# A new order for the last three groups of a planned kernel: by the path that each operation has left, instead of group by group

## The chip, the cores and the metric

The kernel runs on one core of a Trainium2 chip. The metric is the device time of one launch in microseconds (us), a median of several runs. A core has five engines with instruction streams of their own: TensorE (PE in the profile, with its weight loads as PEld), VectorE (DVE), ScalarE (ACT), GpSimd (POOL) and SyncE (SP), which here only issues DMA transfers. Each engine takes its instructions strictly in the order in which the program lists them; between engines they wait for each other by semaphores. So the order of the list is a thing that can be tuned by itself.

## The reference

The input x has 128 graphs of 64 nodes with 256 features (8192 rows of 256 floats), and all share one 64x64 adjacency matrix. Four layers follow, each on a normalised input and added to x:

```
h = relu(layernorm(x));  x = x + layer0(h, adj)   # two graph convolutions, then LSTMs over windows of 1..4 graph nodes
h = relu(layernorm(x));  x = x + layer1(h, adj)   # normalised Laplacian, 4-head masked attention, Gelu MLP, layer norms
h = relu(layernorm(x));  x = x + layer2(h, adj)   # graph attention: softmax of leaky relu of s1 + s2, masked
h = relu(layernorm(x));  x = x + layer3(h, adj)   # U^T h, a two-layer MLP, U h; U = eigenvectors of a Laplacian of adj
```

Layer 1 needs the largest eigenvalue of adj, and layer 3 all eigenvectors of a matrix made from it. Both depend on adj alone. No row of one graph meets another graph's rows after layer 0's windows are closed within the graph, so the work can be cut into groups of graphs freely.

## The kernel before

The kernel records every operation first, with the buffers that it reads and writes, and gives each a group number. Group -1 is the set-up, groups 0 to 7 are layer 0 on eight parts of x, 8 and 9 load the weights of the later layers, and groups 10 to 25 are layers 1 to 3 on sixteen parts of 512 rows each. The eigen-decomposition is a group of its own, set aside, and fills gaps of the other engines during layer 0.

```python
NT, GT, HT = 64, 8, 4                  # (put together) tiles of 128 rows; tiles of a layer-0 group; tiles of a later group
NG = NT // GT                          # 8
NEARLY = 6
ORDER = [g % NG for g in range(NG - NEARLY, 2 * NG - NEARLY)]
SETUP, WEIGHTS, ATTN, REST, EIG = -1, NG, NG + 1, NG + 2, 1000
...
    for i, g in enumerate(ORDER):
        plan.group = REST + 2 * i
        x = X[g]
        if g < len(put):
            x = load(back[g], put[g])
        for h in range(GT // HT):
            plan.group = REST + 2 * i + h
            xh = x[:, h * HT:(h + 1) * HT, :]
            layer1(xh)
            layer2(xh)
            layer3(xh)
            SP.dma_start(xout[g * GT // HT + h], xh)
    plan.issue()
```

Then a planner plays the recorded operations through with a modelled cost for each, and writes down the order in which they start; that order is the program. At each step it looks on every engine at the operations whose inputs are there. One that can start at once comes before one that has to wait, and among those that can start at once the rank decides, the smallest first:

```python
    def schedule(self):
        for op in reversed(self.ops):
            op.path = op.lat + max((o.path for o in op.after), default=0.0)
        ...
        while len(order) < len(self.ops):
            oldest = min(left)
            best = None
            for e, ops in ready.items():
                pick = None
                for op in ops:
                    if op.group != self.aside and op.group >= oldest + self.window(oldest):
                        continue
                    t = max(now[e], op.ready)
                    ...                # and a free buffer of each kind, some kept back for the oldest group
                    rank = (t > now[e] + 1e-9, t if t > now[e] + 1e-9 else 0.0, self.rank(op))
                    if pick is None or rank < pick[0]:
                        pick = (rank, t, op)
                if pick and (best is None or pick[1] < best[1]):
                    best = pick
            ...

    def rank(self, op):
        if op.group == self.aside:
            return (-2 if op.eng == "PE" else 1000, op.index)
        return (op.group, -op.path, op.index)
```

`op.path` is the length of the longest chain of operations that starts with this one, in modelled us: what is left to the end along that chain. So an operation of an older group always goes first, and within one group the one with the longest chain. How many groups may be open at once, and what is kept back for the oldest, is set here:

```python
    def window(oldest):
        return max(oldest, 0) + 2 - oldest if oldest < NG - 1 else max(oldest, REST) + 6 - oldest

    def reserve(kind, oldest):
        if oldest < NG:
            return {"big": 4, "mid": 6, "stat": 1, "attn": 0, "bank": 3}[kind]
        return {"big": 6, "mid": 0, "stat": 2, "attn": 1, "bank": 2}[kind]
```

With the oldest unfinished group at 10 or later, six groups are open. The kinds are buffers: "big" is a wide one in SBUF (128 x 1032 floats), "stat" holds statistics, "attn" a block-diagonal attention matrix, and "bank" is one of the eight PSUM banks. The list of big buffers grows as places fall free; each place is named with the groups that must be done before:

```python
NBIG, NMID, NSTAT, NATTN = 8, 8, 14, 4
    ...
    more(arena[:, (NG - NEARLY) * GT * D:], (EIG,))
    more(whh[3], tuple(range(NG)))
    more(mids, tuple(range(NG)))
    ...
    for i, g in enumerate(ORDER[:NEARLY]):
        more(places[g % NEARLY], (REST + 2 * i, REST + 2 * i + 1))
```

The three layers of one group, cut to their stages (every line stands for several instructions; the first layer is by far the longest):

```python
    def layer1(x):
        h = relu_norm(x); lx = mix_fm(h, lapb)                      # VectorE, GpSimd, ScalarE; then 16 products on TensorE
        x1 = tm(); ... proj_tm(lx, Wc); norm(x1); ...
        x1T = to_fm(x1)                                             # transposes on TensorE
        qT, kT, v = ...                                             # 3 projections
        ps = [bank("qk") for m in range(2)]
        with plan.burst(): ...                                      # 32 products of 64x64, one unbroken run
        s = ...; softmax; pT = fm(); ...                            # Exp on ScalarE, transposes
        with plan.burst(): ...                                      # 32 products of 64x64
        x2 = ... Wo ...; norm(x2); x2T = ...                        # projection, layer norm, transposes
        mT = ... AF.Gelu ...                                        # W1, Gelu on ScalarE
        ps = proj_tm(mT, W2, 4, t0); ...; norm(x2); x += ...        # W2, layer norm

    def layer2(x):
        hT = to_fm(relu_norm(x)); wh = tm(HT, D + 2); ...           # transposes, projection to 258 columns
        V.tensor_mul(s2d, ...); PE.matmul(ps, same, flat(s2d)); ... # the sum s1 + s2
        V.tensor_scalar(e2, e, 0.2, ...); softmax; Exp; transposes
        ... PE.matmul(..., pT, wh) ...; x += ...

    def layer3(x):
        h = relu_norm(x); aT = mix_fm(h, Ub)
        hid = ... W3a ...; uT = ... UTb ...; x += ... W3b ...
```

Of the kernel before, what the change touches and what calls it, by code (L numbers as in the profile page):

```python
# [19 lines left out]
class Virt:  # L20
# [3 lines left out]
    def __init__(self, val, ap, path=()):  # L24
        self.val, self.ap, self.path = val, ap, path
# [41 lines left out]
class Plan:  # L67
# [5 lines left out]

    SLACK = {"PE": 0.12, "V": 0.05, "ACT": 0.05, "G": 0.05, "SP": 0.05}

    def __init__(self, tc, engines, pools, late, reserve, window, aside):

        self.tc, self.engines, self.pools, self.late = tc, engines, pools, late
        self.reserve, self.window, self.aside = reserve, window, aside
        self.ops, self.group, self.seen = [], 0, {}
        self.run, self.whole = None, False

# [129 lines left out]
    def schedule(self):  # L215
# [17 lines left out]
# [9 lines that stand above are left out]
                    need = {}  # L242
                    for v in op.vals:
                        if v.buf is None:
                            need[v.kind] = need.get(v.kind, 0) + 1
                    for k, c in need.items():
                        spare = 0
                        if op.group != oldest:
                            spare = max(0, self.reserve(k, oldest) - held.get((k, oldest), 0))
                        times = sorted(free[k].values())  # L250
                        t = max(t, times[c - 1]) if len(times) >= c + spare else None
                        if t is None:
                            break
                    if t is None:
# [6 lines that stand above are left out]
# [44 lines left out]
    def rank(self, op):  # L305
        if op.group == self.aside:
            return (-2 if op.eng == "PE" else 1000, op.index)
        return (op.group, -op.path, op.index)

    def issue(self):  # L310
        real = lambda a: a.real() if isinstance(a, Virt) else a
# [540 lines left out]
NT = 64  # L852
GT = 8
NG = NT // GT
HT = 4
# [3 lines left out]
SETUP, WEIGHTS, ATTN, REST, EIG = -1, NG, NG + 1, NG + 2, 1000  # L859
# [37 lines left out]
def gnn_kernel(ctx: ExitStack, tc: tile.TileContext, a, out):  # L897
    nc = tc.nc
# [3 lines left out]
    def C(shape, name):  # L902
        return pool.tile(list(shape), F32, name=name)
# [6 lines left out]
    pools = {  # L910
        "big": [C([P, HT * (D + 2)], f"big{i}") for i in range(NBIG)],
        "mid": [mids[:, i * 512:(i + 1) * 512] for i in range(NMID)],
        "stat": [C([P, HT * 10], f"stat{i}") for i in range(NSTAT)],
        "attn": [wih[3][:, i * HT * P:(i + 1) * HT * P] for i in range(NATTN)],
        "bank": [psum.tile([P, 512], F32, name=f"bank{i}") for i in range(8)],
    }
    late = {("attn", i): (ATTN,) for i in range(NATTN)}
# [17 lines left out]
            return {"big": 4, "mid": 6, "stat": 1, "attn": 0, "bank": 3}[kind]  # L935
        return {"big": 6, "mid": 0, "stat": 2, "attn": 1, "bank": 2}[kind]

    plan = Plan(tc, {"PE": nc.tensor, "V": nc.vector, "ACT": nc.scalar, "G": nc.gpsimd, "SP": nc.sync}, pools, late, reserve, window, EIG)
    PE, V, ACT, G, SP = (plan.proxy(e) for e in ("PE", "V", "ACT", "G", "SP"))

    def bank(name):
# [587 lines left out]
```

## Time and profile before

The median of three runs is 2389.2 us (2388.43 to 2390.73). The profiled execution has a span of 2386.6 us and 33035 instructions.

| engine | busy, us | share of the span | instructions |
|---|---|---|---|
| PE (TensorE) | 2291.3 | 96% | 11288 |
| PEld (its weight loads, beside PE) | 1604.7 | 67% | 11288 |
| DVE (VectorE) | 1742.6 | 73% | 6943 |
| ACT (ScalarE) | 974.9 | 41% | 1939 |
| POOL (GpSimd) | 458.5 | 19% | 448 |

All operations are issued by one line of the planner (line 316), so the rows of the profile are told apart by engine, by shape and by the names of the buffers, and not by line. "arena", "x", "mids", "Wih" and "Whh" are places in SBUF: weights and parts of x of layer 0 lay there first, and the buffers and weights of the later layers take the places over. So a name tells where an operand lies and not what it is; the shape and the number of instructions tell that. One float32 product shows as two matmul instructions, a transpose as one. In rows of the timeline the columns are the start, the duration, engine, line, operation, output and input, the partitions and columns, the number of instructions merged, and in square brackets the idle time of the engine before them with what ended it. "PEclk", or the granted clock, is the share of its full clock that TensorE was given.

### The profile page before, as it was taken

The page shows a single profiled execution, that of the slowest core. Times are in us where ns is not written, and L with a number is a line of the kernel's source. Part 1 is how long each engine was busy: PE and PEld are TensorE (multiplying, and loading weights), DVE is VectorE, ACT ScalarE, POOL GpSimd, SP SyncE. Part 2 cuts the span into 40 slices and gives each one's busy share as a digit, 9 for nine tenths or more (in the row PEclk, how much of TensorE's full clock was granted, in tenths as well). Part 3 has the DMA queues.
Part 4 walks back from the last instruction along what each step waited for, and adds up shares of the span by engine and source line. Part 5 has one row for each costly group of instructions (what it writes and reads, how often), then busy time and mean ns, then how long its engine had stood idle before and what let it go on. Part 6 is the DMA issues. An engine that isn't in the chain of part 4 may idle for free. (4 is left out here: it accounts for less than half of the span.)

```text
span 2386.6 us, 33035 instructions
## 1 busy us (share of the span) xinstructions
PE 2291.3 (96%) x11288; PEld 1604.7 (67%) x11288; DVE 1742.6 (73%) x6943; ACT 974.9 (41%) x1939; POOL 458.5 (19%) x448
## 2 busy tenths in 40 slices
PE   8999999999999999999999999999999999999885
PEld 6577477478477477576576577767767777677664
DVE  7656657667999999999886236678568768867653
ACT  3333433433333433333333423555545455545442
POOL 2101001001001001001001023234244433533321
PEclk9999999999999999999999999999999999999998
DMA  6000001000000000000000110000000001000000
GB/s 238 1 1 18 1 1 54 0 1 1 1 1 1 1 1 1 1 1 5 1 1 3 36 35 1 1 10 10 10 18 10 1 27 36 10 10 9 10 10 18
DMA packets 27384, 35.44 MB, mean 15 GB/s; under 512 B 3280, under 2 KB 24656, under 8 KB 26704
## 3 DMA queue, kind: packets, MB, share of 16 engines
q1 hardware_dynamic: 27216, 33.34, 4.2%
q8 instruction: 89, 1.46, 0.3%
q14 instruction: 79, 0.65, 0.1%
HBM read 22.85 MB, written 10.49 MB: 14 GB/s over the span
## 5 line engine op out<-in xcount | busy, mean ns | idle before, releaser
L316 PE MATMUL bank<-big,Wih 128*128 128x256 f32 (+2 forms) x2592 | 867.5, 476 | 7.2 <-DVE Wih L316 2.1
L316 PEld LDWEIGHTS bank<-big,Wih 128*128 128x128 f32 x2592 | 480.6, 191 | 280.9 <-issue 164.7
L316 ACT ACTIVATE mids<-bank,bl 128x256 f32<-128x256 f32 (+2 forms) x624 | 344.5, 563 | 618.0 <-PE bank L316 608.9
L316 PE MATMUL bank<-big,Whh 128*128 128x256 f32 (+2 forms) x1440 | 453.0, 449 | 0.0
L316 DVE TENSOR_TENSOR arena<-arena 64x21 f32<-64x21 f32 (+6 forms) x2317 | 377.1, 193 | 35.4 <-POOL arena L316 1.1
L316 PEld LDWEIGHTS bank<-big,Whh 128*128 128x128 f32 x1440 | 269.1, 190 | 119.1 <-issue 61.5
L316 POOL TENSOR_TENSOR stat<-stat,mhalf 128x4 f32<-128x4 f32 x112 | 116.2, 1038 | 727.8 <-DVE stat L316 726.0
L316 DVE TENSOR_TENSOR big<-big,mids 128x256 f32<-128x256 f32 (+2 forms) x192 | 93.9, 489 | 156.3 <-ACT mids L316 155.1
L316 DVE TENSOR_TENSOR big<-mids 128x512 f32<-128x512 f32 (+2 forms) x244 | 139.8, 579 | 32.2 <-ACT mids L316 28.1
L316 ACT ACTIVATE mids<-big 128x256 f32<-128x256 f32 (+2 forms) x176 | 89.9, 511 | 133.5 <-DVE big L316 78.2
L316 PE MATMUL bank<-Wih,big 128*128 128x256 f32 (+2 forms) x552 | 134.3, 389 | 0.8 <-ACT big L316 0.5
L316 DVE TENSOR_SCALAR arena<-arena 64x1 f32<-64x1 f32 (+5 forms) x597 | 122.7, 212 | 9.3 <-POOL arena L316 1.3
L316 PEld LDWEIGHTS bank<-Wih,big 128*128 128x128 f32 x552 | 104.1, 196 | 20.1 <-issue 3.2
L316 ACT COPY big<-bank 128x512 f32<-128x512 f32 (+1 forms) x129 | 67.8, 559 | 92.5 <-PE bank L316 88.5
L316 PE MATMUL bank<-arena,Whh 128*128 128x512 f32 (+2 forms) x288 | 100.9, 489 | 0.0
L316 POOL TENSOR_TENSOR arena<-arena 64x1 f32<-64x1 f32 x66 | 43.1, 654 | 299.2 <-ACT arena L316 166.2
L316 ACT ACTIVATE mids<-x,stat 128x256 f32<-128x256 f32 x100 | 52.1, 591 | 102.9 <-PE bank L316 48.2
L316 DVE SCALAR_TENSOR_TENSOR arena<-arena 64x1 f32<-64x1 f32 (+4 forms) x391 | 85.3, 223 | 8.7 <-POOL arena L316 3.7
L316 DVE BATCH_NORM_STATS2 stat<-x 128x6 f32<-128x256 f32 x240 | 87.8, 410 | 2.3 <-DMA x<-in_x_dram 2.3
L316 PE MATMUL bank<-Whh,big 128*128 128x256 f32 (+1 forms) x392 | 84.3, 360 | 1.4 <-ACT big L316 1.3
L316 PEld LDWEIGHTS bank<-adjTb,mids 128*128 128x128 f32 x512 | 68.2, 195 | 20.6 <-issue 15.7
L316 PEld LDWEIGHTS bank<-Whh,big 128*128 128x128 f32 x392 | 68.3, 194 | 16.6 <-issue 5.8
(323 smaller groups left out, 3330.4 us busy)
## 6 DMA issues: line engine op xcount, KB each, us to landing
x<-in_x_dram SPq DMA_DIRECT2D x7, 1024.0 KB, 11.6
out_dram<-x SPq DMA_DIRECT2D x12, 512.0 KB, 2.9
Wih<-in_WihT_dram SPq DMA_DIRECT2D x3, 1024.0 KB, 11.1
Whh<-in_WhhT_dram SPq DMA_DIRECT2D x3, 1024.0 KB, 12.8
put<-x SPq DMA_DIRECT2D x2, 1024.0 KB, 4.4
arena<-put SPq DMA_DIRECT2D x2, 1024.0 KB, 5.8
out_dram<-arena SPq DMA_DIRECT2D x4, 512.0 KB, 2.9
x<-in_x_dram SPq DMA_DIRECT2D x4, 256.0 KB, 6.8
```

The costliest lines, as they stand in the source:

```text
L316: getattr(self.engines[op.eng], name)(*map(real, args), **{k: real(a) for k, a in kw.items()})
```

## The change

The planner gets one more number, `ends`, the first of the last groups whose ranks are merged. It is set to REST + NT // HT - 3 = 10 + 16 - 3 = 23, so that groups 23, 24 and 25 are concerned.

```diff
-    def __init__(self, tc, engines, pools, late, reserve, window, aside):
+    def __init__(self, tc, engines, pools, late, reserve, window, aside, ends):
...
-        self.reserve, self.window, self.aside = reserve, window, aside
+        self.reserve, self.window, self.aside, self.ends = reserve, window, aside, ends
...
     def rank(self, op):
         if op.group == self.aside:
             return (-2 if op.eng == "PE" else 1000, op.index)
-        return (op.group, -op.path, op.index)
+        g = min(op.group, self.ends)
+        return (g, 8 * (op.group - g) - op.path, op.index)
...
-    plan = Plan(tc, {...}, pools, late, reserve, window, EIG)
+    plan = Plan(tc, {...}, pools, late, reserve, window, EIG, REST + NT // HT - 3)
```

For groups up to 22 the rank is what it was. Groups 23, 24 and 25 share the first key, 23. Among their operations the one with the longest chain left goes first, where 8 us are taken off the chain for group 24 and 16 us for group 25. The three groups are meant to go through their layers nearly side by side, each 8 us behind the one before, so that they finish nearly together and the engines don't run out of independent work when only the last group is left. What is computed stays the same, and so do the buffers, the window and the costs in the planner.

More of the change, by code (lines that the diff above doesn't have):

```diff
@@ L936, in reserve @@
         return {"big": 6, "mid": 0, "stat": 2, "attn": 1, "bank": 2}[kind]
-    plan = Plan(tc, {"PE": nc.tensor, "V": nc.vector, "ACT": nc.scalar, "G": nc.gpsimd, "SP": nc.sync}, pools, late, reserve, window, EIG)
+    plan = Plan(tc, {"PE": nc.tensor, "V": nc.vector, "ACT": nc.scalar, "G": nc.gpsimd, "SP": nc.sync}, pools, late, reserve, window, EIG, REST + NT // HT - 3)
     PE, V, ACT, G, SP = (plan.proxy(e) for e in ("PE", "V", "ACT", "G", "SP"))
```

## The prediction

> **What bounds the kernel now.** I read four views in this order: busy shares, the stores of the results, the busy time by stretch at the end, and the instructions of TensorE there.
>
> The busy shares of the whole span come first:
>
> ```profile
> PE 2291.3 (96%) x11288; PEld 1604.7 (67%) x11288; DVE 1742.6 (73%) x6943; ACT 974.9 (41%) x1939; POOL 458.5 (19%) x448
> ```
>
> TensorE is busy 96% of 2386.6 us; the second engine, VectorE, 73%. A new order of the same instructions can win only what TensorE doesn't do: its idle time, and the time in which its matmuls run slowly. So I look for where these are. The last four stores on the queue of SyncE close groups 22, 23, 24 and 25:
>
> ```profile
> 2235.77 0.37 SPq L316 DMA_DIRECT2D out_dram<-arena  x1
> 2275.73 0.37 SPq L316 DMA_DIRECT2D out_dram<-arena  x1
> 2341.03 0.37 SPq L316 DMA_DIRECT2D out_dram<-arena  x1
> 2382.58 0.37 SPq L316 DMA_DIRECT2D out_dram<-arena  x1
> ```
>
> The groups end one after another, 40, 65 and 42 us apart. From 2275.7 only two groups live, from 2341.0 only one. In the stretches between these marks (columns: length, then busy us of TensorE, weight loads, VectorE, ScalarE, GpSimd, granted clock, DMA):
>
> ```profile
> 2260.00:2275.00 15.00, 15.00 (x138) 12.57 (x137) 7.96 (x23) 5.51 (x11) 4.39 (x3) 1.00 0.00 1
> 2275.00:2291.60 16.60, 16.60 (x66) 11.61 (x65) 5.73 (x11) 7.89 (x12) 4.74 (x3) 1.00 0.09 32
> 2291.60:2341.00 49.40, 39.19 (x234) 28.62 (x232) 29.34 (x82) 21.76 (x39) 10.58 (x8) 0.93 0.00 1
> 2341.00:2347.20 6.20, 0.00 (x0) 0.00 (x0) 4.38 (x14) 1.30 (x4) 1.01 (x1) 0.82 0.25 85
> 2347.20:2366.00 18.80, 13.44 (x38) 8.84 (x38) 5.97 (x15) 6.00 (x11) 0.86 (x1) 0.70 0.00 0
> 2366.00:2381.20 15.20, 9.50 (x48) 8.62 (x48) 3.42 (x12) 3.15 (x6) 3.37 (x2) 0.78 0.00 1
> ```
>
> Up to 2291.6 TensorE is full. Then it idles 10.2 us beside two groups, 6.2 us with nothing at all, and 5.4 and 5.7 us beside the last group alone: 27.5 us between 2275 and 2381.2. The reader should also see the seventh figure: the clock falls to 0.70 to 0.82. The instructions of TensorE show what that costs; each pair below is the same work, first of group 24, then of group 25 alone (second layer's projection, then the last layer's mixing):
>
> ```profile
> 2309.41 3.75 PE L316 MATMUL bank<-Wih,mids 128*128 128x258 f32 x16 [0.56 <-ACT mids L316]
> 2330.07 1.95 PE L316 MATMUL bank<-Ub,arena 128*128 128x128 f32 x16
> 2347.25 2.17 PE L316 MATMUL bank<-ident,big 128*128 128x128 f32 x8 [7.26 <-ACT big L316]
> 2349.88 6.36 PE L316 MATMUL bank<-Wih,big 128*128 128x258 f32 x16 [0.46 <-ACT big L316]
> 2369.89 3.78 PE L316 MATMUL bank<-Ub,big 128*128 128x128 f32 x16 [3.98 <-ACT big L316]
> ```
>
> 3.75 became 6.36 us and 1.95 became 3.78 us, each behind a long wait. So the loss at the end is idle time plus matmuls at a low clock. The waits of TensorE from 2275 to 2382 name the chain that leaves it idle, the evacuations and normalisations of a single group:
>
> ```profile
> PE bank L316 <- ACT big L316: 13.6, 5, 7.3
> PE bank L316 <- ACT Wih L316: 3.8, 2, 3.2
> PE bank L316 <- DVE arena L316: 3.6, 2, 2.8
> ```
>
> All rows of that view sum to 27.2 us. The same view from 2021 to 2275, with more groups alive, sums to 15.1 us in 254 us, or 5.9%.
>
> **What the Trainium skill says.** "Perfetto Trace Analysis", section "Optimization Strategy", says that a kernel may have regimes with different busiest engines, and that interleaving them can help. The trace agrees on the premise: the chains of one group and the matmuls of another fit beside each other up to 2291.6 and no longer after. "TensorE: Matmul & The Clock Gate", section "What's actually happening", says that the array falls to half its clock after an idle window of about 3.4 us and needs a window of work to get back. The pairs above agree: 3.78 against 1.95 us is a ratio of 1.94, behind a wait of 3.98 us. "SBUF — State Buffer", section "SBUF: two separate sides", says that GpSimd and certain VectorE instructions lock each other out for a whole instruction. The trace agrees: the scaling of the second layer's scores takes 2.28 us at 2315.96, while a GpSimd addition of 2.35 us runs from 2315.74, and 0.29 us at 2358.44 without one. "ScalarE: Activation LUTs", section "What ACT_TABLE_LOAD costs", gives about 1283 ns for a load of a table. In the trace 13 of them after 2021 have a mean of 1283 ns.
>
> **The change part by part.** It adds and removes no instruction by itself; the number of table loads may move by a few, as Gelu and Exp of different groups mix. It changes one sort key of the planner. Groups 23, 24 and 25 get the same first key, and within them the operation with the longest remaining path goes first, with 8 us subtracted for group 24 and 16 us for group 25. Groups 10 to 22 keep their order among themselves and their precedence over the last three.
>
> First, where it can act. Group 24 may start when the oldest unfinished group is 19, and group 25 when it is 20, thus after the stores at 2020.6 and 2071.2 us. Up to about 2020 the two kernels should agree instruction for instruction. Between there and 2180, when group 21 is stored, five or six groups are active and TensorE is short of time, not of work. I count no change there. From there on the three groups share what group 22 leaves, so 23 should end later than 2275.7, and 24 and 25 sooner.
>
> Second, the work left. I cut at 2275, since TensorE lost little before it. After it TensorE is busy 16.6 + 39.2 + 13.4 + 9.5 = 78.7 us. Of this, slow clock is: the output projection at 2299.19 (6.08 us for 16 matmuls, 3.61 us at 2094.68) 2.5; two sets of eight transposes (1.92 and 2.17 against 1.04) 2.0; the 128x258 projection (6.36 against 3.67 at 2076.72) 2.7; the attention product at 2362.36 (3.55 against 1.89) 1.7; the mixing 1.8; the last hidden layer's 16 (2.92 against 1.95 at 2060.14) 1.0. The sum is 11.7, which leaves 67.0 us of work at full clock.
>
> Third, what idles in the new order. (a) The ordinary rate of 5.9% on 71 us of TensorE time: 4.2 us. (b) The end of group 25. From 2366.0 to 2381.2 the last layer idles 5.7 us of 15.2. The stagger of 8 us covers the first half with group 24, but the other groups' matmuls don't come exactly when wanted; I keep the whole 5.7. (c) A squeeze. Layers two and three are a chain of about 40 us (2341 to 2381), with about 8.0 + 6.8 = 14.8 us of matmuls at full clock (transposes 1.04 and 0.66, projection 3.67, score 0.70, product 1.89; mixing 1.95, hidden 1.95, back 1.05, output 1.89). With the three groups 8 us apart, the last 40 us hold 14.8 + 14.8 x 32/40 + 14.8 x 24/40 = 35.5 us of matmuls. TensorE and the chain are then nearly equally long, and when two limits are that close each lengthens the other. I allow 4 us.
>
> TensorE thus ends at 2275 + 67.0 + 4.2 + 5.7 + 4 = 2355.9 us. From its end to the end of the span it was 2386.6 - 2381.2 = 5.4 us (last addition, store, closing waits), which stays. This gives a span of 2361.3. The measured time was 2389.2 against a profiled span of 2386.6, so 2.6 more: 2363.9. I predict 2364 us, some 25 us or 1.1% less.
>
> **The rivals.** First, *buffers hold the three apart*. Three groups in attention want about six wide SBUF buffers each (x1, its transpose, q, k, v, scores), and six more stay reserved for the oldest group: 18 + 6 = 24. The code has 8 + 5 + 1 + 3 = 17, and one more for each finished pair, so 23 from 2180 on. It is close. If group 25 still trails by a third of a group, it ends alone for some 15 us more, and about half of the gain goes: 2376. Against it: groups at different places hold fewer, and after attention only four.
>
> Second, *the plan and the chip part ways*. The order on each engine is fixed from modelled costs. With three groups interleaved finely, an operation that is late on VectorE (the 2.28 us above) holds back the other groups' operations behind it. The tail's idle time then comes back as many short waits: at 10% instead of 5.9% over the 176 us from 2180, 7 us more, or 2371; if the work up to 2275 is disturbed likewise, 2380 to 2390. For it: VectorE is busy 8 to 9 tenths of some of the 10 us stretches between 2180 and 2210, just where three groups would meet. Against it: six groups were already interleaved from 2021 to 2275 at 5.9%.
>
> Third, *everything works better than I allow*: no squeeze, and the last layer half covered. This takes off (c) and half of (b), 6.9 us: 2357. The floor is 2275 + 67.0 + 5.4 + 2.6 = 2350 us.
>
> **Range and chances.** The floor makes 2350 the natural lower end, and the mild forms of the first two rivals reach 2371 to 2380. I take 2353 to 2382. A gain of 2% means 2341.4 us, 9 us under the floor, and could come only from waits before 2275 that vanish too: 1 in 100. A loss of 2% means 2437 us, for which some 48 us of new stalls would have to arise in the last 370 us: 1 in 100.
>
> **What would show each step right or wrong.** Up to about 2020 us the stores fall at the same times. The stores of groups 23, 24 and 25 move together: 23 to some 2335, 24 to 2347, 25 to 2358, instead of 2275.7, 2341.0 and 2382.6. TensorE's granted clock stays near 1.00 until the last 20 us, and the 128x258 projection of the last group takes under 4 us, not 6.36. The idle time of TensorE from 2275 to its end is about 14 us instead of 27.5. I am wrong if the stores still lie over 30 us apart (first rival), if TensorE idles notably more than 6% between 2100 and 2300 (second), or if the clock still falls in the last 40 us although three groups live (then the chain of one layer, common to all three, is the limit and not the lack of a second group).

## The result, and the profile after

The changed kernel takes 2354.67 us (2353.95 to 2356.87, four runs); beside it the kernel before took 2389.97 us. The ratio is 0.9847, with a 95% interval of 0.9825 to 0.9870. The prediction was 2364 us in a range of 2353 to 2382: the direction and the mechanism held, and the gain is 35.3 us where about 25 was predicted. The time lies only 1.7 us above the lower end of the range. The profiled execution has a span of 2352.2 us, 34.4 less than before.

The busy shares of the page of the changed kernel split these 34.4 us at once:

```profile
PE 2280.0 (97%) x11288; PEld 1599.4 (68%) x11288; DVE 1740.0 (74%) x6943; ACT 971.4 (41%) x1935; POOL 457.3 (19%) x448
```

The same 11288 matmul instructions keep TensorE busy for 2280.0 us instead of 2291.3. These 11.3 us are matmuls that run faster. The rest, 34.4 - 11.3 = 23.1 us, is idle time that is gone. The waits of TensorE tell where. From 2275 us to the end they were 27.2 us and are 9.2; from 2180 to 2275 they were 7.4 and are 2.3; from 2000 to 2180 they were 7.8 and are 7.2.

Nothing of the gain is older than 2129 us. The first 9914 of the 11288 instructions of TensorE are the same in both programs, and the next one starts at 2129.35 us before and at 2129.34 us in the changed kernel. There 16 transposes stand in a row before (L316), while in the changed kernel (L319) a mixing follows after eight of them:

```profile
2128.48 1.91 PE L316 MATMUL bank<-ident,mids 128*128 128x128 f32 x16
2128.46 1.04 PE L319 MATMUL bank<-ident,mids 128*128 128x128 f32 x8
2129.34 1.95 PE L319 MATMUL bank<-lapb,x 128*128 128x128 f32 x16
```

The stores that close groups 22 to 25, on the queue of SyncE of the changed kernel:

```profile
2228.86 0.37 SPq L319 DMA_DIRECT2D out_dram<-arena  x1
2329.70 0.37 SPq L319 DMA_DIRECT2D out_dram<-arena  x1
2338.47 0.37 SPq L319 DMA_DIRECT2D out_dram<-arena  x1
2348.21 0.37 SPq L319 DMA_DIRECT2D out_dram<-arena  x1
```

Group 22 ends 6.9 us sooner than before, group 23 ends 54 us later, 24 and 25 end 2.6 and 34.4 us sooner, and the last three lie 9 and 10 us apart. The stretches of the changed kernel after 2275 us (columns as before):

```profile
2275.00:2291.60 16.60, 16.60 (x70) 11.42 (x69) 8.76 (x23) 10.51 (x19) 4.79 (x4) 1.00 0.01 1
2291.60:2310.00 18.40, 14.47 (x71) 12.17 (x70) 16.76 (x59) 10.55 (x21) 4.28 (x4) 0.96 0.00 0
2310.00:2320.00 10.00, 8.79 (x52) 7.42 (x52) 7.49 (x20) 5.88 (x12) 3.48 (x2) 0.91 0.01 2
2320.00:2330.00 10.00, 9.56 (x64) 8.75 (x63) 7.30 (x16) 4.53 (x10) 4.22 (x3) 1.00 0.00 0
2330.00:2340.00 10.00, 8.01 (x47) 6.20 (x45) 6.62 (x20) 3.15 (x7) 2.01 (x2) 1.00 0.22 74
2340.00:2347.00 7.00, 5.29 (x32) 4.34 (x32) 1.53 (x3) 0.58 (x2) 1.35 (x1) 1.00 0.14 46
```

The 6.2 us with no matmul at all are gone, and the clock stays at 1.00 in the last 27 us of matmuls, where it was 0.70 to 0.82. It dips in the middle instead, within the two stretches from 2291.6 to 2320 (0.96 and 0.91), and only for the length of one mixing: from 2312 on it is 1.00. Ahead of the dip VectorE is busy 16.76 of 18.40 us, and the three groups are between the end of their first layer and their third. The instructions of TensorE of the changed kernel around that place:

```profile
2305.67 0.70 PE L319 MATMUL bank<-arena,same 128*128 128x256 f32 x2 [1.58 <-DVE arena L319]
2308.72 3.55 PE L319 MATMUL bank<-Ub,x 128*128 128x128 f32 x16 [2.35 <-ACT x L319]
...
2319.21 3.75 PE L319 MATMUL bank<-Wih,x 128*128 128x258 f32 x16
```

The mixing at 2308.72 still runs slowly (3.55 us, 1.95 at full clock), behind two holes of 1.58 and 2.35 us. The projection of the last group at 2319.21 no longer does (3.75 us, 6.36 before).

### The profile page after: what moved, and what is told of

Same layout as the page of the kernel before. It is cut to its first block, busy times and chain, and to the rows that moved or that the text cites. A ratio compares the mean times of both kernels' runs of the same rounds, so it can differ in the third digit from the quotient of the medians.

```text
span 2352.2 us, 33030 instructions
## 1 busy us (share of the span) xinstructions
PE 2280.0 (97%) x11288; PEld 1599.4 (68%) x11288; DVE 1740.0 (74%) x6943; ACT 971.4 (41%) x1935; POOL 457.3 (19%) x448
## 4 chain that ended last, share of the span: by engine, by line
PE 80%; DVE 15%; ACT 2%; issue 1%; POOL 1%; DMA 0%; SPq 0%; DVEq 0%; ACTq 0%; POOLq 0%
PE bank L319 80%; DVE stat L319 4%; DVE big L319 4%; DVE arena L319 3%; DVE x L319 1%; DVE mids L319 1%; DVE Whh L319 1%; ACT big L319 1%; ACT arena L319 1%; POOL stat L319 0%; ACT mids L319 0%; DMA x<-in_x_dram 0%; ACT Wih L319 0%; POOL mids L319 0%; DVE Wih L319 0%
## 5 line engine op out<-in xcount | busy, mean ns | idle before, releaser
L319 PE MATMUL bank<-big,Wih 128*128 128x256 f32 (+2 forms) x2592 | 865.6, 475 | 5.7 <-DVE Wih L319 2.1
L319 PEld LDWEIGHTS bank<-big,Wih 128*128 128x128 f32 x2592 | 479.3, 190 | 278.1 <-issue 164.2
L319 ACT ACTIVATE mids<-bank,bl 128x256 f32<-128x256 f32 (+2 forms) x624 | 344.5, 563 | 617.3 <-PE bank L319 608.1
L319 PE MATMUL bank<-big,Whh 128*128 128x256 f32 (+2 forms) x1440 | 453.4, 449 | 0.0
L319 DVE TENSOR_TENSOR arena<-arena 64x21 f32<-64x21 f32 (+6 forms) x2314 | 374.8, 192 | 35.3 <-POOL arena L319 1.1
L319 PEld LDWEIGHTS bank<-big,Whh 128*128 128x128 f32 x1440 | 269.0, 190 | 118.2 <-issue 61.0
L319 POOL TENSOR_TENSOR stat<-stat,mhalf 128x4 f32<-128x4 f32 x112 | 117.5, 1050 | 709.7 <-DVE stat L319 707.7
L319 DVE TENSOR_TENSOR big<-big,mids 128x256 f32<-128x256 f32 (+2 forms) x192 | 93.9, 489 | 155.4 <-ACT mids L319 154.2
L319 DVE TENSOR_TENSOR big<-mids 128x512 f32<-128x512 f32 (+2 forms) x244 | 140.0, 579 | 32.2 <-ACT mids L319 28.1
L319 ACT ACTIVATE mids<-big 128x256 f32<-128x256 f32 (+2 forms) x176 | 89.9, 511 | 133.5 <-DVE big L319 78.2
L319 DVE TENSOR_SCALAR arena<-arena 64x1 f32<-64x1 f32 (+5 forms) x598 | 122.9, 212 | 9.3 <-POOL arena L319 1.3
L319 PE MATMUL bank<-Wih,big 128*128 128x256 f32 (+1 forms) x488 | 116.1, 382 | 0.3 <-DVE mids L319 0.3
L319 PE MATMUL bank<-arena,Whh 128*128 128x512 f32 (+2 forms) x304 | 108.9, 494 | 0.5 <-DVE arena L319 0.5
L319 PEld LDWEIGHTS bank<-Wih,big 128*128 128x128 f32 x488 | 90.3, 192 | 17.6 <-issue 4.3
L319 POOL TENSOR_TENSOR arena<-arena 64x1 f32<-64x1 f32 x66 | 43.1, 654 | 299.7 <-ACT arena L319 166.8
L319 ACT COPY big<-bank 128x512 f32<-128x512 f32 (+1 forms) x127 | 65.6, 549 | 75.7 <-PE bank L319 71.9
L319 ACT ACTIVATE mids<-x,stat 128x256 f32<-128x256 f32 x100 | 52.1, 591 | 103.1 <-PE bank L319 48.2
L319 DVE SCALAR_TENSOR_TENSOR arena<-arena 64x1 f32<-64x1 f32 (+4 forms) x391 | 85.3, 223 | 8.7 <-POOL arena L319 3.7
L319 DVE COPY arena<-bank 64x1 f32<-64x1 f32 (+23 forms) x185 | 37.1, 202 | 66.4 <-PE bank L319 58.1
L319 PE MATMUL bank<-Whh,big 128*128 128x256 f32 (+1 forms) x384 | 83.4, 360 | 2.5 <-ACT big L319 1.5
L319 DVE BATCH_NORM_STATS2 stat<-x 128x6 f32<-128x256 f32 x228 | 83.8, 410 | 2.3 <-DMA x<-in_x_dram 2.2
L319 PEld LDWEIGHTS bank<-adjTb,mids 128*128 128x128 f32 x512 | 68.8, 197 | 20.6 <-issue 15.9
## 6 DMA issues: line engine op xcount, KB each, us to landing
x<-in_x_dram SPq DMA_DIRECT2D x7, 1024.0 KB, 11.7
```

What stands on the lines that cost most here:

```text
L319: getattr(self.engines[op.eng], name)(*map(real, args), **{k: real(a) for k, a in kw.items()})
```

## The experiments

"Theory A" and "theory B" are two readings of the result. A: it is enough that three independent groups are alive to the end. B: they must also stand at different stages, so the offset of 8 us does the work. Each set of runs has its own runs of the kernel before; the ratio is to these. The profiled executions differ by up to 9 us already in the stretch that all these programs share (the last section shows one cause). So where two profiled spans are compared below, the text says how far apart they stood when their programs parted: at the first instruction of TensorE that differs.

| kernel | time, us | ratio to before, 95% interval |
|---|---|---|
| changed kernel | 2354.67 | 0.9847 (0.9825 to 0.9870) |
| three groups, no offset | 2413.27 | 1.0084 (1.0065 to 1.0104) |
| two groups, 8 us | 2375.51 | 0.9935 (0.9910 to 0.9960) |
| three groups, youngest first | 2364.73 | 0.9886 (0.9864 to 0.9908) |
| six groups, 5 us | 2347.93 | 0.9812 (0.9794 to 0.9830) |
| before, holes filled | 2382.16 | 0.9961 (0.9948 to 0.9973) |
| changed, holes filled | 2355.83 | 0.9847 (0.9833 to 0.9862) |
| three groups, 16 us | 2383.20 | 0.9964 (0.9950 to 0.9978) |
| six groups, 5 us, holes filled | 2352.87 | 0.9823 (0.9802 to 0.9843) |
| changed kernel again | 2355.47 | 0.9844 (0.9825 to 0.9864) |
| six groups, 8 us | 2359.19 | 0.9868 (0.9845 to 0.9891) |
| three groups, 5 us | 2362.82 | 0.9868 (0.9847 to 0.9890) |
| six groups, 5 us, again | 2346.58 | 0.9807 (0.9787 to 0.9826) |

**No offset.**

```diff
-        return (g, 8 * (op.group - g) - op.path, op.index)
+        return (g, 0 * (op.group - g) - op.path, op.index)
```

> The changed kernel with the offset of 8 us per group set to 0: groups 23, 24 and 25 are ranked by the path left alone, so that they go in step. Theory A (the gain comes from three independent groups being alive to the end, whatever their distance): the three stores fall within 10 us of each other and the time is that of the changed kernel or a little less, 2345 to 2360 us. Theory B (the gain comes from the groups standing at different stages, and the offset is what makes them): in step, all three want TensorE in the same stage and leave it idle in the same stage; idle time of TensorE after 2180 us of 40 us and more instead of some 12, with the clock falling in each hole, and 2395 to 2430 us, slower than the kernel before.

It is slower than the kernel before, by 0.84%, and 58.6 us slower than the changed kernel. The three stores lie 1.2 us apart, and after 2180 us TensorE waits 49.8 us, where the changed kernel has 11.5. The profiled execution is 25.0 us longer than that of the kernel before; 5.6 of these were lost before the programs parted (2088.2 against 2082.6 us), so 19.4 are the order's. The stretches of this kernel:

```profile
2310.00:2320.00 10.00, 10.00 (x48) 8.79 (x47) 0.78 (x2) 0.00 (x0) 0.00 (x0) 1.00 0.01 2
2320.00:2330.00 10.00, 1.25 (x6) 0.76 (x4) 8.16 (x34) 0.93 (x2) 2.24 (x3) 0.73 0.00 1
2330.00:2340.00 10.00, 0.00 (x0) 0.00 (x0) 9.81 (x21) 5.09 (x11) 0.74 (x1) 0.50 0.00 0
```

First TensorE works nearly alone, then VectorE and, in part of the time, ScalarE work without it. The instruction of TensorE that ends the hole names whom it waited for:

```profile
2344.43 1.68 PE L319 MATMUL bank<-ident,arena 128*128 128x128 f32 x6 [23.18 <-ACT arena L319]
```

What VectorE does in these 23 us is the same work three times over. In its timeline three groups' normalisations are merged in single rows:

```profile
2337.58 4.02 DVE L319 BATCH_NORM_STATS2 stat<-arena 128x6 f32<-128x256 f32 x12
2341.51 0.90 DVE L319 BATCH_NORM_AGGREGATE stat<-stat 128x2 f32<-128x6 f32 x12
2342.31 0.30 DVE L319 TENSOR_SCALAR stat<-stat 128x4 f32<-128x4 f32 x3
```

A group alone has four of the first and second kind and one of the third. Three groups in step make one group of three times the size, whose stages follow one another. Theory A falls and B holds: three groups alive to the end were worth nothing here while all wanted the same engine.

**Two groups.**

```diff
-... EIG, REST + NT // HT - 3)
+... EIG, REST + NT // HT - 2)
```

> The changed kernel with only the last two groups, 24 and 25, sharing a rank, 8 us apart. Group 23 ends by itself as in the kernel before, at some 2276 us. Both theories: with two groups in the last 100 us TensorE idles less than with one and more than with three; about half of the gain, 2366 to 2377 us. A third group that adds nothing would give 2353 to 2358 us.

As expected, and by the medians a little under half of the gain, 15.6 us. From 2275 us on TensorE waits 16.1 us, between 27.2 and 9.2. This execution stood level with the other two when the programs parted (2129.29 us), and its span is 2369.7 us: 16.9 less than that of the kernel before and 17.5 more than that of the changed kernel. So the third group adds as much as the second.

**Youngest first.** The offset is -8 instead of 8.

> The changed kernel with the sign of the offset turned: the youngest of the three groups is 16 us ahead and the oldest last. Theory B (only the distance matters): within 5 us of the changed kernel, 2350 to 2360 us, and the stores come in the order 25, 24, 23. Rival C (the oldest must lead, because buffers are kept back for it alone and it has a start): 10 us or more slower, 2364 to 2385 us.

Neither band was hit cleanly: 2364.73 us is 10 us over the changed kernel, at the edge of rival C. The profile speaks against C all the same. Its span is 7.5 us longer than that of the changed kernel, and 3.4 of these were lost before the two programs parted (2084.39 against 2080.99 us). From 2283.74 us on, TensorE has the same sequence of shapes as the changed kernel, 5.0 us later (the first 128x258 projection starts at 2288.81, there at 2283.84), and the waits after 2275 us are 9.2 us in both. So 1.6 us were lost where the order differs. The last 2.5 us are clock: behind the same holes the matmuls run slower for longer than in the changed kernel, where the same stretch, 5 us earlier, has 0.91:

```profile
2315.00:2325.00 10.00, 8.72 (x35) 7.36 (x34) 5.11 (x11) 4.78 (x10) 3.47 (x2) 0.51 0.01 2
```

The distance does for the end what it did before. The stores lie 9 and 10 us apart as in the changed kernel; which group each of them closes, the names in the trace don't tell. Of the difference between 7.5 us in the profiled spans and 10 us in the medians I have no account.

**The clock by itself.** In the kernel before, idle matmuls fill the holes that its plan foresees on TensorE in the last three groups. Each writes the place that the next matmul overwrites, so nothing real moves and no buffer is taken. There are 101 of them, or 202 instructions.

```diff
             for op in order:
+                if op.eng == "PE":
+                    out = real(op.calls[0][1][0])
+                    if REST + 13 <= op.group < EIG and len(op.calls) == 1 and out.shape[0] == P and op.t - pe > 0.5 and op.calls[0][2].get("start", True):
+                        n = min(out.shape[-1], 256)
+                        each = 0.00084 * 2 * n + 0.01
+                        for _ in range(int((op.t - pe - 0.3) / each)):
+                            self.engines["PE"].matmul(out[:, :n], self.warm[0], self.warm[1][:, :n], start=True, stop=True)
+                    pe = op.t + op.cost
```

> The kernel before, in the same order, with idle matmuls put into the holes of TensorE in groups 23 to 25: where the plan has a hole of over 0.5 us ahead of a matmul, dummy matmuls of constants fill it but for 0.3 us, writing the place that the matmul overwrites next. No real work moves. Theory (the low clock behind the holes is a part of the loss of its own, some 11.7 us after 2275 us): the 128x258 projection at the end takes 3.7 us instead of 6.36, the mixing 1.95 instead of 3.78, and the time falls by 6 to 11 us, to 2379 to 2385 us. Rival (the slow matmuls lie beside waits that are as long anyway, or the dummies come in the way of the real ones): 2387 us or more.

The time falls by 0.39%, some 9 us. The instructions of TensorE of this kernel (L321 are the idle ones):

```profile
2345.86 7.53 PE L321 MATMUL bank<-B1T,ident 128*128 128x128 f32 x66
2353.29 1.91 PE L324 MATMUL bank<-ident,big 128*128 128x128 f32 x8
2355.04 0.60 PE L321 MATMUL bank<-B1T,ident 128*128 128x256 f32 x2
2355.77 3.75 PE L324 MATMUL bank<-Wih,big 128*128 128x258 f32 x16
```

The last projection takes 3.75 us instead of 6.36, and the last mixing 2.19 instead of 3.78. This execution was already 8.4 us behind the kernel before when its W1 products of group 24 began (2286.47 against 2278.07), and 1.2 us behind when its last matmuls began (2380.78 against 2379.56). So the clock alone is worth 7.2 us of the tail. The transposes keep their 1.91 us at full clock: the four activations that feed them take 2.08 us together, so they are paced by these and not by the clock.

> The same filling in the changed kernel. Its plan has few holes left, nine of over 0.5 us, and the mixing at 2308.72 (3.55 us against 1.95) and its followers are the only slow ones: 0 to 4 us less than the changed kernel, 2350 to 2357 us. If it were 8 us or more faster, the clock would still be a main loss there.

In the changed kernel the filling gives nothing, 2355.83 us: its profiled execution is 1.7 us behind that of the changed kernel before the programs part, and 1.7 us behind at the end. Little slow work on the chain is left there.

**More offset.** 16 instead of 8.

> The changed kernel with an offset of 16 us instead of 8, so 16 and 32 us in all. Theory B (the offset must part the stages but each us of it leaves the last group alone at the end): the stores lie some 20 us apart, group 25 is alone for the last 16 to 20 us and the clock falls there; 2366 to 2382 us, between the changed kernel and the kernel before. Rival (more distance is as good or better): 2358 us or less.

At 2383.2 us it is slightly over the band of theory B. The waits of TensorE after 2180 us sum to 29.7 us, against 11.5 in the changed kernel (2.3 + 9.2). Group 24 is stored at 2355.34 us, so group 25 has the last 21 us of matmuls to itself, and from 2360 on the clock is 0.77. So for three groups the best offset lies between 0 and 16 us: too little and the groups move in step, too much and the last one is alone again.

**More groups.** The last six groups, 5 us apart, by

```diff
-        return (g, 8 * (op.group - g) - op.path, op.index)
+        return (g, 5 * (op.group - g) - op.path, op.index)
-... EIG, REST + NT // HT - 3)
+... EIG, REST + NT // HT - 6)
```

> The last six groups (20 to 25) share a rank, 5 us apart. If the squeeze at the end of the changed kernel (TensorE idle for some 9 us after 2291 us) and the waits before it come from too few different stages being open, more groups at more stages fill them: 2340 to 2350 us. If the plan and the chip part ways as more groups are mixed, short waits on TensorE spread over 2000 to 2340 us and the time is 2355 us or more.

At 2347.93 us it lies in the first band and beats both kernels. To see which half of the edit does it, four kernels ran on one chip:

> The changed kernel once more, as the measure for the other three of this set on the same chip: 2352 to 2358 us.

> Six groups share a rank, the offset stays at 8 us (40 us in all): the number of groups alone is changed. If the number brings the gain of six groups 5 us apart, 2345 to 2350 us; if it is the offset, 2352 to 2358 us as the changed kernel.

> Three groups share a rank, the offset is 5 us instead of 8: the offset alone is changed. If a shorter offset brings the gain (the last group is alone for 3 us less), 2347 to 2352 us; if three groups 5 us apart lie closer to the same stage and wait more in the middle, 2353 to 2360 us, nothing gained.

> Six groups, 5 us apart, beside the changed kernel on one chip: 5 to 9 us less than it, with intervals that don't meet.

Six groups 5 us apart took 2346.58 us and the changed kernel 2355.47. The runs of the one (2345.36 to 2349.19) and of the other (2354.14 to 2357.5) don't overlap, though the intervals of the two ratios to before just touch (0.9825 and 0.9826). Neither half gives this alone: six groups at 8 us and three at 5 us are 4 and 7 us slower than the changed kernel, both outside what was expected of them. The 4 us are the order's: that execution was 0.7 us behind the changed kernel when the programs parted, at 1890 us, and 5.1 at the end (with six groups at 5 us it was 0.7 behind there and 8.6 ahead at the end). Most of the 7 us are not. Up to the mixing at 2129.34 us three groups at 5 us and the changed kernel have the same program, and there the profiled execution was already 7.2 us late:

```profile
2136.58 1.95 PE L319 MATMUL bank<-lapb,x 128*128 128x128 f32 x16
```

At the end it is 8.8 us late, so the shorter offset alone cost some 1.6 us. From 2275 us on TensorE waits 9.2 us in the changed kernel, 9.5 with six at 8 us, 9.2 with three at 5 us, and 4.3 with six at 5 us. The stretches of this last kernel show the place where the others dip:

```profile
2291.60:2310.00 18.40, 18.40 (x121) 17.00 (x120) 16.00 (x49) 11.85 (x25) 8.44 (x7) 1.00 0.09 30
2310.00:2320.00 10.00, 9.36 (x68) 8.59 (x67) 9.13 (x26) 4.10 (x9) 1.80 (x2) 1.00 0.15 52
```

TensorE is full there, since groups 20 to 22 have work left (their stores come in the last 50 us). Why the two halves need each other was not settled; a list planned greedily can also move by a few us from one setting to the next for no deeper reason.

> The last six groups 5 us apart, with the holes of groups 23 to 25 filled by dummy matmuls as well. If both losses are separate, some 1 to 4 us less than without the filling (2347.9): 2344 to 2347 us. If no slow matmuls are left there, no difference.

The filling brings nothing there either; at 2352.87 us, with runs from 2345.18 to 2353.66, it can't be told from 2347.93. The profiled execution was 4.9 us behind that of six groups at 5 us without the filling when the order of the list began to differ from the kernel before (1898.8 against 1893.9 us), and 4.7 at the end.

## Why the prediction held, and where its sum was off

**Where the change acts.** Right. The programs part at 2129 us, and the first ten stores of the later groups lie within 2 us of each other. These 2 us are not order, since the program is the same there, and they are gone at the eleventh store, at 2117.6 us in both.

**The work left at 2275 us.** This term was mis-sized. The prediction took 67.0 us of full-clock work as left, since TensorE lost little before 2275. But the kernel before had lost 7.4 us to waits between 2180 and 2275, and the changed one lost 2.3: with three groups at different stages there was nearly always one with a product ready (with two groups it lost 6.4, with three in step 14.5). The prediction named such waits only as the way to a gain of 2%, at 1 in 100. With these 5.1 us TensorE had more of its work done at 2275, and was busy for 62.7 us after it instead of 67.0, slow matmuls included.

**What idles in the new order.** I allowed 4.2 + 5.7 + 4 = 13.9 us, and the sum is 9.2, of which nine holes make 9.0. Term (a), ordinary stalls: none at all up to 2304 us. Term (c), the squeeze: 1.58 + 2.35 + 0.45 + 0.64 + 0.44 = 5.5 us between 2304 and 2330, where 4 was allowed. The squeeze came as described, but with VectorE as the engine that is nearly full (16.76 of 18.40 us from 2291.6 on) while three chains of one kind meet; the prediction had set TensorE against one chain. Term (b), the end of group 25: 1.53 + 0.45 + 0.78 + 0.78 = 3.5 us instead of 5.7: the hole of 3.98 us ahead of its mixing is filled by the last two products of group 24 (the second at 2335.50), but for the 1.53. The two errors, 4.3 us of work and 4.7 of idle time, are the 9 us by which the span of 2352.2 missed the 2361.3 of the sum.

**The slow clock.** Its part in the loss was right in kind. 11.7 us were read off pairs of rows; TensorE's busy time fell by 11.3 over the whole span. But 2.0 us of the pairs were transposes that wait for their inputs, and of the rest 7.2 reached the end, as the filled holes show. I also expected the clock to stay near 1.00 until the last 20 us, which failed for the mixing at 2308.72 and held in the last 20 us themselves. From 2312 us on, thus in the last 40 us, the clock is 1.00, so the sign named against the mechanism did not appear.

**The rivals.** Buffers didn't hold the groups apart: the stores lie 9 and 10 us from each other, close to the offset. Plan and chip didn't part ways: the waits fell after 2180 us and hardly moved from 2000 to 2180. The third rival, better than allowed, came nearest, with 2357 us. What none of the rivals had was the danger that the lockstep run shows. I took the offset of 8 us as a detail of the last layer, where it carries the whole gain.

## What to carry to other kernels

When one engine is full in the body of a kernel, look at its end: here the last piece of work ran alone, its chain left holes, and the matmuls behind them ran at a clock of 0.70 to 0.82. Let the last few pieces overlap, but keep them apart by part of a stage: with three groups 8 us gained 35 us here, 0 us lost 20, 16 us gained 9. And when the gain is estimated, count the holes of the whole stretch in which the new order acts, not only those of the last piece. When two orders are compared by profiles, find the first instruction that differs and subtract what one execution was ahead there: it was up to 9 us here.

## What the hardware showed that I had not expected

The place where the clock falls isn't fixed by the program. About 1400 us, before the two programs differ, the same 16 and 18 matmuls of 128x256 follow holes of 1.44 and some 2.1 us. In the kernel before they took 3.72 and 5.84 us, in the changed kernel 3.72 and 4.15, and in its second profiled run 5.41 and 4.15, with the hole between them shorter in turn (0.45 us). So these matmuls can take some 1.7 us more in one execution than in another. Less than half of that lasted here, since waits behind them become shorter in turn: the kernel before was 0.3 us ahead of the changed one at 1322 us and 0.4 us behind at 1454 us. "TensorE: Matmul & The Clock Gate", section "What's actually happening", has the window free-running, which fits; it puts the fall after an idle window of about 3.4 us, while here holes of 1.58 and 2.35 us with 0.7 us of work between them were enough (the mixing at 2308.72).

A larger loss comes from VectorE and GpSimd. Of the 14 profiled executions five (three groups in step, six groups at 5 us with and without the filling, before with the filling, three groups at 5 us) fell 3.5 to 4.7 us behind that of the changed kernel between 1805 and 1838 us, where all programs are the same. The first pair of rows is from the changed kernel, the second from three groups at 5 us:

```profile
1819.54 0.41 DVE L319 TENSOR_TENSOR Whh<-Whh,stat 128x256 f32<-128x256 f32 x1
1820.83 2.37 POOL L319 TENSOR_TENSOR arena<-arena,Whh 128x1024 f32<-128x1024 f32 x1 [1.76 <-PE bank L319]
1823.37 2.56 DVE L319 TENSOR_TENSOR Whh<-Whh,stat 128x256 f32<-128x256 f32 x1
1822.97 2.67 POOL L319 TENSOR_TENSOR arena<-arena,Whh 128x1024 f32<-128x1024 f32 x1
```

In the five, the addition on GpSimd starts 0.4 us before the subtraction on VectorE, which then takes 2.56 us; in the other nine it starts 1.3 to 1.4 us after it, and the subtraction takes 0.41 us. TensorE waits behind the long subtraction (0.61 and 2.71 us in three groups at 5 us) and not at all behind the short one. What parts the five from the nine is the row of 20 matmuls of TensorE just before: it takes 4.48 us in all of the five and 5.18 to 6.17 us in the nine. In the nine GpSimd waits for TensorE there, as in the second row; so the faster row lets its addition start ahead of the subtraction on VectorE, and the execution loses more than the row has won.
